# Experts: Silu on ScalarE, clip and sum on GpSimd, features on partitions in the down projection, token weights spread through DRAM

## The chip, the core and the metric

The kernel runs on one core of a Trainium2 chip. The metric is the device time of one execution in microseconds (us). TensorE is written PE below, VectorE DVE, ScalarE ACT, GpSimd POOL and SyncE SP.

## What is computed

The input x has 8 sequences of 512 tokens with 128 features. The reference, cut to what matters here:

```python
h = _layernorm(x) * (1 + ca) + sa
x = x + ga * attn(h)             # gates by softmax, then a scan over the 512 time steps
h = _layernorm(x) * (1 + cb) + sb
# ffn(h): 8 experts, 4 of them chosen per token
logits = x @ router_weight.T + router_bias
topk_w = softmax(top_k(logits, 4))
combine = zeros((N, E)).at[arange(N)[:, None], topk_idx].set(topk_w)
gate_up = einsum('nd,ejd->nej', x, gate_up_proj) + gate_up_proj_bias
gate, up = split(gate_up, 2, axis=-1)
gate = minimum(gate, 7.0)
up = clip(up, -7.0, 7.0)
act = (up + 1.0) * gate * sigmoid(1.702 * gate)
out = einsum('nei,edi->ned', act, down_proj) + down_proj_bias
y = einsum('ned,ne->nd', out, combine)
x = x + gb * y
```

Every expert is computed for every token; the weights of the experts that a token did not choose are 0. An expert has 256 hidden features. All data are float32.

## The kernel before

**Tiles.** A tile is 16 time steps of all 8 sequences, 128 tokens. There are 32 tiles. Four tiles make a superchunk (512 tokens, `NW`), and there are 8 superchunks.

**The stages.** `ln1(s)` normalises a superchunk. `gates(c)` makes the softmax gates of a tile: five matmuls (L220), for each a maximum and a subtraction on DVE (L224, L226) and an Exp on ACT (L229); then a sum, a reciprocal and a product over 2176 elements on DVE (L234, L235, L238). Eight DMAs from SP's queue (L243, 136 KB each) carry the gates to a layout with one row per head and sequence. `scan(c)` runs the 16 steps of a tile on DVE, one product (L256) and one sum (L259) per step, each waiting for the one before. `attn_out(c)` carries the states back with eight small DMAs (L269) and multiplies by W_out. `attn_post(s)` adds the residual, normalises, and makes the router: logits (L300), ranks, and the token weights `comb` (L338), tokens on partitions. It then transposes `comb` on PE (L345), copies it to `cT` (L347), and starts `y` with the weighted output biases (L350, L355).

**The experts.** `experts(s, es)` works through pairs of expert e and half ic of its 256 features, 16 to a superchunk. `front` issues two matmuls of 128x512 (gate L365, up L367), copies both from PSUM with their biases on ACT (L371, L373), and takes the Sigmoid of the gate copy (L375). `back` clips up on DVE (L382), multiplies by the limited gate (L383) and by the limited Sigmoid (L384); the result is `act`. `down` multiplies by the down projection with `act` as the stationary operand, so that tokens lie on the partitions of the output: 4 blocks of tokens times 2 halves, 8 matmuls of 128 columns (L391), each of which the profile shows as two instructions. Its PSUM tile `pd` has a single buffer (`ps_dn`, bufs=1). `combine` adds the output to `y` with the token weight as a per-partition scalar, four instructions on DVE (L399):

```python
nc.vector.scalar_tensor_tensor(
    y[:, k, :], pd[:, k, :], comb[:, k, e : e + 1], y[:, k, :], ALU.mult, ALU.add
)
```

`finish` multiplies `y` by the modulation row (L427), adds `x1` (L428), and stores (L431). The final `y` is tokens by features.

**What sets the order.** The functions are generators. Beside the scan of tile c the main loop advances `attn_out(c - 1)`, `ln1`, `gates(c + 2)` and a quarter of the experts of the superchunk before. From this text a scheduler makes a fixed order for each engine when the kernel is built, with an estimate of each instruction's length; it also places the waits, and each engine then works through its own list strictly in order. In the built order the experts of a superchunk do not lie evenly beside the scan: they stand together in a burst after `comb`, with a few scan steps between them, and the gates and most scan steps follow. A DMA is issued from the list of the engine that its line names, and a wait before it holds up that list. The DMAs of SP and ACT share eight completion semaphores in turn, so that a DMA also waits for the one that used its semaphore last.

Of the kernel before, what the change touches and what calls it, by code (L numbers as in the profile page):

```python
# [9 lines left out]
F32 = mybir.dt.float32  # L10
AF = mybir.ActivationFunctionType
ALU = mybir.AluOpType
AX = mybir.AxisListType

P = 128
EPS = 1e-5
ALPHA = 1.702
LIMIT = 7.0
TOP_K = 4
SIG_MAX = 1.0 / (1.0 + math.exp(-ALPHA * LIMIT))  # L20

# [7 lines left out]
def adaln_block_kernel(  # L29
    ctx: ExitStack,  # L30
    tc: tile.TileContext,
    x: bass.AP,        # [B, T, D]
    norm_w: bass.AP,   # [D, 1]
    wa_t: bass.AP,     # [D, H*M*(M+1)]
    wv_t: bass.AP,     # [D, D]
    wo_t: bass.AP,     # [D, D]
    rw_t: bass.AP,     # [D, E]
    r_bias: bass.AP,   # [1, E]
    gu_t: bass.AP,     # [D, E*2I]
    gu_bias: bass.AP,  # [128, E*4]  # L40
    dn_t: bass.AP,     # [E, I, D]
    dn_bias: bass.AP,  # [E, D]
    c_in: bass.AP,     # [B, D]
    w_mod: bass.AP,    # [D, 6*D]
    out: bass.AP,      # [B, T, D]
):
# [24 lines left out]
    ps_gu = ctx.enter_context(tc.tile_pool(name="ps_gu", bufs=3, space=PS))  # L71
    ps_dn = ctx.enter_context(tc.tile_pool(name="ps_dn", bufs=1, space=PS))
    ps_misc = ctx.enter_context(tc.tile_pool(name="ps_misc", bufs=2, space=PS))

    def misc_psum(name):
        return ps_misc.tile([P, 512], F32, tag="misc", name=name)

# [1 line left out]
    c_sb = const.tile([B, D], F32, name="c_sb")  # L79
# [31 lines left out]

# [1 line left out]
    ident = const.tile([P, P], F32, name="ident")  # L113
# [11 lines left out]
    )  # L125
    # up's bias with the 1 of (up + 1)
    ub1_sb = const.tile([P, E, IC], F32, name="ub1_sb")
    nc.vector.tensor_scalar(ub1_sb, gub_sb[:, :, IC:], 1.0, None, ALU.add)

# [1 line left out]
    sig_c = const.tile([B, D], F32, name="sig_c")  # L131
# [8 lines left out]
    for half in range(2):  # L140
# [5 lines left out]
            start=True, stop=True,  # L146
# [11 lines left out]
    def mod_row(i):  # L158
        return mod[:, i, :].unsqueeze(1).to_broadcast([P, KT, D])

# [1 line left out]
    def layernorm(dst, src, scale_i, shift_i, tag):  # L162
# [23 lines left out]
    f_tiles = {}      # superchunk -> what the experts need  # L186

# [96 lines left out]
    def attn_post(s):  # L284
        r = r_tiles.pop(s)
        x1 = sc_p.tile([P, KT, D], F32, tag="x1", name=f"x1_{s}")
        nc.vector.tensor_tensor(r, r, mod_row(2), ALU.mult)
        nc.vector.tensor_tensor(x1, r, x_sb[:, s * KT : (s + 1) * KT, :], ALU.add)
        h2 = sc_p.tile([P, KT, D], F32, tag="h2", name=f"h2_{s}")
        yield from layernorm(h2, x1, 4, 3, "b")  # L290
# [5 lines left out]
        yield  # L296
        # router: top 4 of 8, softmax over the chosen
        pr = misc_psum(f"pr{s}")
# [42 lines left out]
        yield  # L341
        # the experts' output biases, weighted
        pc = misc_psum(f"pc{s}")
# [3 lines left out]
        nc.scalar.copy(cT, pc[:E, :])  # L347
        pb = misc_psum(f"pb{s}")
        for k in range(KT):
            nc.tensor.matmul(  # L350
                pb[:, k * D : (k + 1) * D], cT[:, k * P : (k + 1) * P], dnb_sb,
                start=True, stop=True,
            )
        y = sc_p.tile([P, KT, D], F32, tag="y", name=f"y{s}")
        nc.scalar.copy(y.rearrange("p k d -> p (k d)"), pb)  # L355
        f_tiles[s] = (x1, h2T, comb, y)
        yield

    def experts(s, es):
        x1, h2T, comb, y = f_tiles[s]  # L360
        acts = {}

        def front(e, ic):
            pgt = ps_gu.tile([P, NW], F32, tag="gu", name=f"pgt{s}_{e}_{ic}")
            nc.tensor.matmul(pgt, gu_sb[:, e, ic * P : (ic + 1) * P], h2T, start=True, stop=True)  # L365
            pup = ps_gu.tile([P, NW], F32, tag="gu", name=f"pup{s}_{e}_{ic}")
            nc.tensor.matmul(  # L367
                pup, gu_sb[:, e, I + ic * P : I + (ic + 1) * P], h2T, start=True, stop=True
            )
            gt = ffn_p.tile([P, NW], F32, tag="gate", name=f"gate{s}_{e}_{ic}")  # L370
            nc.scalar.activation(gt, pgt, AF.Identity, bias=gub_sb[:, e, ic : ic + 1])  # L371
            up = ffn_p.tile([P, NW], F32, tag="up", name=f"up{s}_{e}_{ic}")
            nc.scalar.activation(up, pup, AF.Identity, bias=ub1_sb[:, e, ic : ic + 1])  # L373
            sg = ffn_p.tile([P, NW], F32, tag="sg", name=f"sg{s}_{e}_{ic}")
            nc.scalar.activation(sg, gt, AF.Sigmoid, scale=ALPHA)  # L375
            return gt, up, sg

        def back(e, ic, gt, up, sg):
            if ic == 0:
                acts[e] = ffn_p.tile([P, IC, NW], F32, tag="act", name=f"act{s}_{e}", bufs=2)  # L380
            # clip(up, -7, 7) + 1, min(gate, 7), sigmoid(1.702 min(gate, 7))
            nc.vector.tensor_scalar(up, up, 1.0 - LIMIT, 1.0 + LIMIT, ALU.max, ALU.min)  # L382
            nc.vector.scalar_tensor_tensor(up, gt, LIMIT, up, ALU.min, ALU.mult)  # L383
            nc.vector.scalar_tensor_tensor(acts[e][:, ic, :], sg, SIG_MAX, up, ALU.min, ALU.mult)  # L384

        def down(e):
            act = acts.pop(e)
            pd = ps_dn.tile([P, KT, D], F32, tag="pd", name=f"pd{s}_{e}")
            for k in range(KT):
                for ic in range(IC):  # L390
                    nc.tensor.matmul(  # L391
                        pd[:, k, :], act[:, ic, k * P : (k + 1) * P], dn_sb[:, e * IC + ic, :],
                        start=(ic == 0), stop=(ic == IC - 1),
                    )
            return pd

        def combine(e, pd):
            for k in range(KT):
                nc.vector.scalar_tensor_tensor(  # L399
                    y[:, k, :], pd[:, k, :], comb[:, k, e : e + 1], y[:, k, :], ALU.mult, ALU.add  # L400
                )

        waiting, downs = None, None
        for e in es:
            for ic in range(IC):
                made = (e, ic, *front(e, ic))
                yield
                if downs is not None:
                    combine(*downs)
                    downs = None  # L410
                if waiting is not None:
                    back(*waiting)
                    if waiting[1] == IC - 1:
                        downs = (waiting[0], down(waiting[0]))
                waiting = made
                yield
        back(*waiting)
        if downs is not None:
            combine(*downs)
        downs = (waiting[0], down(waiting[0]))  # L420
        yield
        combine(*downs)
        yield

    def finish(s):
# [81 lines left out]
```

## Time and profile before

| | us |
|---|---|
| median of the runs before | 1391.12 (three runs, 1390.35 to 1391.66) |
| span of the profiled execution | 1390.6 |
| DVE busy | 1151.2 (83%) |
| PE busy | 675.7 (49%) |
| ACT busy | 462.8 (33%) |
| POOL busy | 1.1 |
| DMA of the gates, g<-ee, in the chain of work that ended last | 15% of the span |

The profiled execution is one run of its own; its span, from the first to the last instruction, is 0.5 us under the median of the timed runs. The page divides the span in 40 slices and gives the busy share of each engine in tenths, lists groups of equal instructions with their busy time, mean length and the idle time just before them, and follows the chain of work that ended last back from the end. PE's busy time is that of pipelined matmuls whose ends are modelled: two matmuls of 0.59 us each may start 0.43 us apart.

### The profile page before, as it was taken

The numbers are of one execution on the slowest core, as the hardware profiler recorded it, in microseconds if no ns is written. First come the engines' busy times: TensorE is split into PE (matmuls) and PEld (weight loads), VectorE is DVE, ScalarE is ACT, GpSimd is POOL, SyncE is SP. The second block draws the span as 40 slices with busy tenths as digits, with TensorE's granted clock in tenths as the row PEclk, the third lists the DMA queues.
The fourth block names the chain that finished last, engine by engine and source line by source line (L and its number), as shares of the span: only waits on it lengthen the run. The fifth ranks groups of instructions, "written<-read, shape, count | busy, mean of one in ns | idle before, by whom it ended". The sixth has DMA issues, their size and how long they took to land.

```text
span 1390.6 us, 9491 instructions
## 1 busy us (share of the span) xinstructions
PE 675.7 (49%) x2181; PEld 348.3 (25%) x2181; DVE 1151.2 (83%) x2533; ACT 462.8 (33%) x850; POOL 1.1 (0%) x10
## 2 busy tenths in 40 slices
PE   1415049531594237830496315942369414771077
PEld 0101015310262014510153102620135201440044
DVE  3889699996999799996989969897898978888366
ACT  2401037320382115610373203821146102541054
POOL 0000000000000000000000000000000000000000
PEclk9755568865697667965688656976569756795579
DMA  6251514024330325005140242303241041501200
GB/s 199 32 60 14 60 21 49 1 32 45 36 31 10 44 25 65 2 11 63 20 51 0 30 48 33 34 10 38 31 50 17 10 54 20 61 1 21 24 0 8
DMA packets 80248, 47.39 MB, mean 34 GB/s; under 512 B 38064, under 2 KB 79296, under 8 KB 79936
## 3 DMA queue, kind: packets, MB, share of 16 engines
q1 hardware_dynamic: 78640, 42.03, 25.8%
q10 hardware_dynamic: 1552, 4.75, 1.0%
q14 instruction: 38, 0.31, 0.1%
q8 instruction: 18, 0.29, 0.1%
HBM read 6.91 MB, written 2.10 MB: 6 GB/s over the span
## 4 chain that ended last, share of the span: by engine, by line
DVE 40%; PE 32%; DMA 21%; issue 2%; SPq 2%; ACT 2%; DVEq 0%; ACTq 0%
DMA g<-ee 15%; PE pgt L365 9%; PE pd L391 8%; DVE g L256 8%; PE pup L367 8%; DVE ys L259 7%; DVE mx L224 5%; DVE z L234 5%; DMA yt<-ys 4%; PE pg L220 4%; DVE ee L226 4%; DVE ee L238 3%; SPq L243 2%; DVE z L235 2%; DMA x_sb<-in_x_dram 1%
## 5 line engine op out<-in xcount | busy, mean ns | idle before, releaser
L256 DVE TENSOR_TENSOR g<-g,ys 64x256 f32<-64x256 f32 x511 | 211.2, 413 | 107.0 <-DMA g<-ee 60.1
L220 PE MATMUL pg<-wav,hnT 128*128 128x459 f32 (+2 forms) x320 | 221.6, 815 | 133.5 <-DVE ee L226 108.7
L259 DVE TENSOR_REDUCE ys<-g 64x16 f32<-64x272 f32 x512 | 217.1, 424 | 11.3
L273 PE MATMUL py<-ident,yt 128*128 128x128 f32 x32 | 13.7, 427 | 436.5 <-DMA yt<-ys 435.8
L275 ACT COPY ytT<-py 128x128 f32<-128x128 f32 x32 | 8.5, 266 | 513.1 <-PE py L273 513.1
L391 PE MATMUL pd<-dn_sb,act 128*128 128x128 f32 x1024 | 146.6, 291 | 29.8 <-DVE act L384 16.2
L391 PEld LDWEIGHTS pd<-dn_sb,act 128*128 128x128 f32 x1024 | 136.2, 201 | 91.3 <-DVE act L384 36.6
L229 ACT ACTIVATE ee<-ee 128x459 f32<-128x459 f32 (+2 forms) x160 | 89.1, 564 | 201.4 <-DVE ee L226 179.6
L365 PE MATMUL pgt<-h2T,gu_sb 128*128 128x512 f32 x256 | 145.9, 654 | 0.0
L367 PE MATMUL pup<-h2T,gu_sb 128*128 128x512 f32 x256 | 138.8, 625 | 0.0
L220 PEld LDWEIGHTS pg<-wav,hnT 128*128 128x128 f32 x320 | 68.9, 254 | 257.2 <-issue 163.1
L273 PEld LDWEIGHTS py<-ident,yt 128*128 128x128 f32 x32 | 6.2, 193 | 461.3 <-issue 302.2
L224 DVE TENSOR_REDUCE mx<-pg 128x27 f32<-128x459 f32 (+2 forms) x160 | 95.1, 594 | 13.5 <-PE pg L220 12.8
L373 ACT ACTIVATE up<-pup,ub_sb 128x512 f32<-128x512 f32 x128 | 86.8, 678 | 40.8 <-PE pup L367 40.8
L371 ACT ACTIVATE gate<-pgt,gub_sb 128x512 f32<-128x512 f32 x128 | 87.6, 684 | 24.7 <-PE pgt L365 24.2
L226 DVE TENSOR_TENSOR ee<-pg,mx 128x459 f32<-128x459 f32 (+2 forms) x160 | 95.2, 595 | 0.0
L384 DVE SCALAR_TENSOR_TENSOR act<-sg,up 128x512 f32<-128x512 f32 x128 | 88.1, 688 | 7.4 <-ACT sg L375 3.4
L383 DVE SCALAR_TENSOR_TENSOR up<-gate,up 128x512 f32<-128x512 f32 x128 | 88.0, 688 | 2.9
L399 DVE SCALAR_TENSOR_TENSOR y<-pd,comb,y 128x128 f32<-128x128 f32 x256 | 74.9, 342 | 14.2 <-PE pd L391 13.9
L375 ACT ACTIVATE sg<-gate 128x512 f32<-128x512 f32 x128 | 80.5, 629 | 2.5
L234 DVE TENSOR_REDUCE z<-ee 128x128 f32<-128x2176 f32 x32 | 76.8, 2400 | 0.5 <-ACT ee L229 0.5
L238 DVE TENSOR_TENSOR ee<-ee,z 128x2176 f32<-128x2176 f32 x32 | 76.9, 2404 | 0.0
(89 smaller groups left out, 599.1 us busy)
## 6 DMA issues: line engine op xcount, KB each, us to landing
g<-ee SPq DMA_DIRECT2D x256, 136.0 KB
yt<-ys SPq DMA_DIRECT2D x256, 8.0 KB
x_sb<-in_x_dram SPq DMA_DIRECT2D x32, 64.0 KB
gu_sb<-in_gu_t_dram ACTq DMA_DIRECT2D x1, 2048.0 KB
out_dram<-y SPq DMA_DIRECT2D x32, 64.0 KB
wav<-in_wa_t_dram ACTq DMA_DIRECT2D x1, 1088.0 KB
wmod_sb<-in_w_mod_dram ACTq DMA_DIRECT2D x1, 384.0 KB
wo_sb<-in_wo_t_dram SPq DMA_DIRECT2D x1, 64.0 KB
```

The source lines that it names most:

```text
L220: nc.tensor.matmul(pg[:, :w], hnT, wav[:, g0 * J : g0 * J + w], start=True, stop=True)
L224: nc.vector.tensor_reduce(mx[:, g0 : g0 + n], pg3, AX.X, ALU.max)
L226: nc.vector.tensor_tensor(e3, pg3, mx[:, g0 : g0 + n].unsqueeze(2).to_broadcast([P, n, J]), ALU.subtract)
L229: nc.scalar.activation(e3, e3, AF.Exp)
L234: nc.vector.tensor_reduce(z, ee, AX.X, ALU.add)
L238: nc.vector.tensor_tensor(ee, ee, z.unsqueeze(2).to_broadcast([P, NG, J]), ALU.mult)
L256: nc.vector.tensor_tensor(a, a, prev.unsqueeze(1).to_broadcast([H * B, M, M]), ALU.mult)
L259: nc.vector.tensor_reduce(ys[:, t, :], g[:, t, :, :], AX.X, ALU.add)
L365: nc.tensor.matmul(pgt, gu_sb[:, e, ic * P : (ic + 1) * P], h2T, start=True, stop=True)
L367: nc.tensor.matmul(pup, gu_sb[:, e, I + ic * P : I + (ic + 1) * P], h2T, start=True, stop=True)
L384: nc.vector.scalar_tensor_tensor(acts[e][:, ic, :], sg, SIG_MAX, up, ALU.min, ALU.mult)
L391: nc.tensor.matmul(pd[:, k, :], act[:, ic, k * P : (k + 1) * P], dn_sb[:, e * IC + ic, :], start=(ic == 0), stop=(ic == IC - 1),)
```

## The change

Seven things change together. (1) ACT takes the Silu of 1.702 times the gate straight from PSUM, with a bias scaled by 1.702 when the kernel starts; the copy of the gate and the Sigmoid go. The limit on the gate becomes a limit on the Silu, and the factor 1.702 that is then too much is divided out of the token weights. (2) The clip of up moves to POOL. (3) On DVE one product per half is left. (4) The down projection has its weights as the stationary operand, so features lie on the partitions of the output and all 512 tokens in its columns: 2 matmuls of 512 columns per expert. (5) The token weights now differ along the columns and are equal in all partitions. They are transposed as before, divided by 1.702 (`cA`), written to DRAM (`cD`, 16 KB) and read back into all 128 partitions (`wB`, 2 MB), both from ACT's queue. (6) Each expert's output is multiplied by its row of `wB` on DVE; POOL adds the products up in `yT`. (7) `finish` turns `yT` back by matmuls with the identity and adds the output biases in the same PSUM tile. Besides, `x1` takes the place of `r`, and some tiles have other numbers of buffers. Comments and blank lines also changed; the diff without them:

```diff
-SIG_MAX = 1.0 / (1.0 + math.exp(-ALPHA * LIMIT))
+SILU_MAX = ALPHA * LIMIT / (1.0 + math.exp(-ALPHA * LIMIT))
...
+    dram = ctx.enter_context(tc.tile_pool(name="dram", bufs=2, space=bass.MemoryType.DRAM))
...
+    gb_sb = const.tile([P, E, IC], F32, name="gb_sb")
+    nc.vector.tensor_scalar(gb_sb, gub_sb[:, :, :IC], ALPHA, None, ALU.mult)
...
-        x1 = sc_p.tile([P, KT, D], F32, tag="x1", name=f"x1_{s}")
-        nc.vector.tensor_tensor(x1, r, x_sb[:, s * KT : (s + 1) * KT, :], ALU.add)
-        h2 = sc_p.tile([P, KT, D], F32, tag="h2", name=f"h2_{s}")
+        nc.vector.tensor_tensor(r, r, x_sb[:, s * KT : (s + 1) * KT, :], ALU.add)
+        x1 = r
+        h2 = sc_p.tile([P, KT, D], F32, tag="h2", name=f"h2_{s}", bufs=1)
...
         cT = small.tile([E, NW], F32, tag="cT", name=f"cT{s}")
         nc.scalar.copy(cT, pc[:E, :])
-        pb = misc_psum(f"pb{s}")
-        for k in range(KT):
-            nc.tensor.matmul(
-                pb[:, k * D : (k + 1) * D], cT[:, k * P : (k + 1) * P], dnb_sb,
-                start=True, stop=True,
-            )
-        y = sc_p.tile([P, KT, D], F32, tag="y", name=f"y{s}")
-        nc.scalar.copy(y.rearrange("p k d -> p (k d)"), pb)
-        f_tiles[s] = (x1, h2T, comb, y)
+        cA = ffn_p.tile([P, NW], F32, tag="w", name=f"cA{s}", bufs=2)
+        nc.scalar.mul(cA[:E, :], pc[:E, :], 1.0 / ALPHA)
+        cD = dram.tile([E, NW], F32, tag="cD", name=f"cD{s}")
+        nc.scalar.dma_start(cD, cA[:E, :])
+        wB = sc_p.tile([P, E, NW], F32, tag="wB", name=f"wB{s}", bufs=1)
+        nc.scalar.dma_start(wB, cD.rearrange("e n -> (e n)").unsqueeze(0).to_broadcast([P, E * NW]))
+        f_tiles[s] = (x1, h2T, cT, wB)
...
-            gt = ffn_p.tile([P, NW], F32, tag="gate", name=f"gate{s}_{e}_{ic}")
-            nc.scalar.activation(gt, pgt, AF.Identity, bias=gub_sb[:, e, ic : ic + 1])
-            up = ffn_p.tile([P, NW], F32, tag="up", name=f"up{s}_{e}_{ic}")
+            sg = ffn_p.tile([P, NW], F32, tag="sg", name=f"sg{s}_{e}_{ic}")
+            nc.scalar.activation(sg, pgt, AF.Silu, bias=gb_sb[:, e, ic : ic + 1], scale=ALPHA)
+            up = ffn_p.tile([P, NW], F32, tag="up", name=f"up{s}_{e}_{ic}", bufs=5)
             nc.scalar.activation(up, pup, AF.Identity, bias=ub1_sb[:, e, ic : ic + 1])
-            sg = ffn_p.tile([P, NW], F32, tag="sg", name=f"sg{s}_{e}_{ic}")
-            nc.scalar.activation(sg, gt, AF.Sigmoid, scale=ALPHA)
-            return gt, up, sg
+            nc.gpsimd.tensor_scalar(up, up, 1.0 + LIMIT, 1.0 - LIMIT, ALU.min, ALU.max)
+            return sg, up
...
-            nc.vector.tensor_scalar(up, up, 1.0 - LIMIT, 1.0 + LIMIT, ALU.max, ALU.min)
-            nc.vector.scalar_tensor_tensor(up, gt, LIMIT, up, ALU.min, ALU.mult)
-            nc.vector.scalar_tensor_tensor(acts[e][:, ic, :], sg, SIG_MAX, up, ALU.min, ALU.mult)
+            nc.vector.scalar_tensor_tensor(up, sg, SILU_MAX, up, ALU.min, ALU.mult)
+            acts.setdefault(e, []).append(up)
...
-            pd = ps_dn.tile([P, KT, D], F32, tag="pd", name=f"pd{s}_{e}")
-            for k in range(KT):
-                for ic in range(IC):
-                    nc.tensor.matmul(
-                        pd[:, k, :], act[:, ic, k * P : (k + 1) * P], dn_sb[:, e * IC + ic, :],
-                        start=(ic == 0), stop=(ic == IC - 1),
-                    )
+            pd = ps_dn.tile([P, NW], F32, tag="pd", name=f"pd{s}_{e}")
+            for ic in range(IC):
+                nc.tensor.matmul(
+                    pd, dn_sb[:, e * IC + ic, :], act[ic],
+                    start=(ic == 0), stop=(ic == IC - 1),
+                )
...
-            for k in range(KT):
-                nc.vector.scalar_tensor_tensor(
-                    y[:, k, :], pd[:, k, :], comb[:, k, e : e + 1], y[:, k, :], ALU.mult, ALU.add
-                )
+            if e == 0:
+                yT_tiles[s] = sc_p.tile([P, NW], F32, tag="yT", name=f"yT{s}", bufs=1)
+                nc.vector.tensor_tensor(yT_tiles[s], pd, wB[:, e, :], ALU.mult)
+                return
+            w = ffn_p.tile([P, NW], F32, tag="w", name=f"w{s}_{e}", bufs=2)
+            nc.vector.tensor_tensor(w, pd, wB[:, e, :], ALU.mult)
+            nc.gpsimd.tensor_tensor(yT_tiles[s], yT_tiles[s], w, ALU.add)
...
-        x1, _, _, y = f_tiles.pop(s)
-        nc.vector.tensor_tensor(y, y, mod_row(5), ALU.mult)
+        x1, _, cT, _ = f_tiles.pop(s)
+        yT = yT_tiles.pop(s)
+        pb = misc_psum(f"pb{s}")
+        for k in range(KT):
+            blk = slice(k * P, (k + 1) * P)
+            nc.tensor.matmul(pb[:, blk], yT[:, blk], ident, start=True, stop=False)
+            nc.tensor.matmul(pb[:, blk], cT[:, blk], dnb_sb, start=False, stop=True)
+        y = sc_p.tile([P, KT, D], F32, tag="y", name=f"y{s}", bufs=1)
+        nc.vector.tensor_tensor(
+            y, pb.rearrange("p (k d) -> p k d", d=D), mod_row(5), ALU.mult
+        )
         nc.vector.tensor_tensor(y, y, x1, ALU.add)
```

More of the change, by code (lines that the diff above doesn't have):

```diff
@@ L186, in adaln_block_kernel @@
     f_tiles = {}
+    yT_tiles = {}
     def ln1(s):
@@ L347, in attn_post @@
         nc.scalar.copy(cT, pc[:E, :])
-        pb = misc_psum(f"pb{s}")
-        for k in range(KT):
-            nc.tensor.matmul(
-                pb[:, k * D : (k + 1) * D], cT[:, k * P : (k + 1) * P], dnb_sb,
-                start=True, stop=True,
-            )
-        y = sc_p.tile([P, KT, D], F32, tag="y", name=f"y{s}")
-        nc.scalar.copy(y.rearrange("p k d -> p (k d)"), pb)
-        f_tiles[s] = (x1, h2T, comb, y)
+        cA = ffn_p.tile([P, NW], F32, tag="w", name=f"cA{s}", bufs=2)
[5 more added lines that the diff above has]
+        f_tiles[s] = (x1, h2T, cT, wB)
         yield
     def experts(s, es):
-        x1, h2T, comb, y = f_tiles[s]
+        x1, h2T, cT, wB = f_tiles[s]
         acts = {}
@@ L373, in front @@
             nc.scalar.activation(up, pup, AF.Identity, bias=ub1_sb[:, e, ic : ic + 1])
-            sg = ffn_p.tile([P, NW], F32, tag="sg", name=f"sg{s}_{e}_{ic}")
-            nc.scalar.activation(sg, gt, AF.Sigmoid, scale=ALPHA)
-            return gt, up, sg
[L378 to L384, printed above, removed]
+            nc.gpsimd.tensor_scalar(up, up, 1.0 + LIMIT, 1.0 - LIMIT, ALU.min, ALU.max)
@@ L386, in down, with back @@
+            return sg, up
+        def back(e, ic, sg, up):
+            nc.vector.scalar_tensor_tensor(up, sg, SILU_MAX, up, ALU.min, ALU.mult)
+            acts.setdefault(e, []).append(up)
         def down(e):
             act = acts.pop(e)
-            pd = ps_dn.tile([P, KT, D], F32, tag="pd", name=f"pd{s}_{e}")
-            for k in range(KT):
-                for ic in range(IC):
-                    nc.tensor.matmul(
-                        pd[:, k, :], act[:, ic, k * P : (k + 1) * P], dn_sb[:, e * IC + ic, :],
-                        start=(ic == 0), stop=(ic == IC - 1),
-                    )
+            pd = ps_dn.tile([P, NW], F32, tag="pd", name=f"pd{s}_{e}")
[4 more added lines that the diff above has]
+                )
```

## The prediction

> **What bounds the kernel now.** I began with the busy line and the 40 slices of the profile page.
>
> ```profile
> PE 675.7 (49%) x2181; PEld 348.3 (25%) x2181; DVE 1151.2 (83%) x2533; ACT 462.8 (33%) x850; POOL 1.1 (0%) x10
> ...
> PE   1415049531594237830496315942369414771077
> ...
> DVE  3889699996999799996989969897898978888366
> ```
>
> VectorE (DVE) is busy 83% of the span and GpSimd (POOL) not at all, so moving work from the first to the second looks like a gain. But TensorE (PE) rises to 9 or 10 tenths once per superchunk: the experts run as a burst. I therefore read the timeline of superchunk 2 (counted from 0) and cut it at three marks: the end of `comb` (L338) at 541.90 us, the first combine (L399) at 549.46, the end of the last at 591.08. The next `comb` ends at 705.96. Busy time in these three stretches (columns: stretch, length, PE, PEld, DVE, ACT, POOL, PE clock, DMA share, GB/s):
>
> ```profile
> 541.90:549.50 7.60, 7.60 (x38) 4.80 (x37) 6.34 (x15) 6.12 (x11) 0.00 (x0) 0.97 0.58 74
> 549.50:591.00 41.50, 36.67 (x167) 23.35 (x166) 37.99 (x98) 29.92 (x54) 0.00 (x0) 0.96 0.11 14
> 591.00:705.90 114.90, 39.87 (x70) 15.64 (x71) 97.30 (x204) 22.35 (x44) 0.00 (x0) 0.62 0.29 34
> ```
>
> A period is 7.6 + 41.5 + 114.9 = 164.0 us. In the last 114.9 us the experts have nothing to do but the final two additions. Only the first 49.1 us are open to this change, and there PE is as full as DVE: 44.3 us of 49.1. The last superchunk, after the scan, shows the burst alone. Its end, in the chain of work that ended last (start, length, what):
>
> ```profile
> 1375.99 1.23 PE pd L391 x11
> 1377.22 0.88 PE pup L367 x2
> 1378.09 0.02 issue
> 1378.12 0.70 ACT up L373
> 1378.81 0.02 issue
> 1378.84 0.44 DVE up L382
> 1379.28 0.02 issue
> 1379.30 0.70 DVE up L383
> 1380.00 0.02 issue
> 1380.03 0.70 DVE act L384
> 1380.73 0.04 issue
> 1380.77 1.84 PE pd L391 x14
> ```
>
> Up to the last expert the chain there is PE matmul on PE matmul. ACT and DVE appear only at the very end.
>
> [...] yt (8 KB) stands in the chain with 1.9 us. [...] with PE nearly idle from 581.6 to 586.1, the clock reads 0.50 from 587 to 590.
>
> **The change part by part.** Groups used (busy us, mean ns):
>
> ```profile
> L384 DVE SCALAR_TENSOR_TENSOR act<-sg,up 128x512 f32<-128x512 f32 x128 | 88.1, 688 | 7.4 <-ACT sg L375 3.4
> L383 DVE SCALAR_TENSOR_TENSOR up<-gate,up 128x512 f32<-128x512 f32 x128 | 88.0, 688 | 2.9
> L399 DVE SCALAR_TENSOR_TENSOR y<-pd,comb,y 128x128 f32<-128x128 f32 x256 | 74.9, 342 | 14.2 <-PE pd L391 13.9
> ```
>
> DVE. Clip (L382, 128 x 423 ns = 54.2 us), first product (L383, 88.0) and combine (L399, 74.9) go: 217 us. Sixty-four products of 128x512 with one PSUM operand come; the nearest rows are 620 ns for 459 elements from PSUM and 688 from SBUF, so 0.68 x 64 = 43.5. Net -174 us of DVE, 21.7 per superchunk. All of it lies in the burst (and the wait for PE is there too), not in the 114.9 us.
>
> ACT. Gate copy (87.6) and Sigmoid (80.5) become one Silu from PSUM, 128 x 684 ns = 87.6: -80 us. The copy of y (0.56) is replaced by cA (0.57). The built order has 58 table loads for 54, +4 x 1.28 us. ACT has 36 us of work in 49: no gain on the path.
>
> PE. An expert's down projection takes 16 short instructions at 0.11 us (14 in 1.56 us) and will take 4 long ones at 0.43 (a pair of pgt lasts 0.86): 1.78 to 1.72 us. No gain worth counting. In `finish` come 8 matmuls per superchunk for 4 removed; they stand among the gates, where PE is busy 39.9 of 114.9 us, and cost nothing except in the last superchunk.
>
> POOL. [...] The clip stands in the place of L382 and L383 (1.1 us), so the chain from ACT to the down projection keeps its length. [...]
>
> The broadcast. This is the new wait. `comb` is transposed, copied twice on ACT, written to DRAM (16 KB), read back into 128 partitions (2 MB); the first combine waits for it, and it stands only some 13 to 18 DVE instructions after `comb`. From the end of `comb`:
> - transposes end at +2.6 (before: 544.56); they keep their place behind a gate matmul.
> - cT and cA, 0.57 each, then up(1,0) 0.68, which stands before the DMA on ACT: +4.6. Issue 0.5 (rows of 0.3 to 0.9 at the start), landing 1.9: +7.0.
> - The read stands on ACT behind Silu(1,1), whose matmul stands behind the first down projection: that begins at +4.5, takes 1.7, the matmul 0.86, Silu 0.69: +7.8. Issue 0.4: +8.2.
> - 2 MB: gu_sb has this size, shape and queue. In its load, 12 to 18 us, 342 GB/s moved on average: 6.1 us, and 1.9 fixed: 8.0. Best, at the 483 GB/s of its fastest microsecond, 6.2; worst 11.6, the time until the next DMA of that queue went out. The gate transfer of the same moment (SP's queue, share 0.58) shares engines, but the built order reuses completion semaphores so that its third and fourth eighths wait for the write and the read; its tile is scanned only after the burst.
> - Landing: +16.2, with bounds +13.5 and +21 (ACT or POOL later).
>
> Before, the first combine was at +7.6. What waits behind it: everything on DVE, in order; and the second down projection, since `pd` has one buffer. PE gets to it at about +10.5 (five matmuls after the first), stops for 6 us, and falls to half clock.
>
> After the landing: product 0.68; on PE 14 down and 21 gate/up matmuls x 0.857 = 30.0; half clock for some 5 us, +2.5; last expert's ACT, POOL, DVE chain 2.3; last product 0.68; handovers 0.3. Sum 36.5. So the last combine ends at 16.2 + 36.5 = +52.7 instead of +49.1: **+3.6 us per superchunk**, x 7 = 25.
>
> In the 114.9 us nothing changes: by the built order DVE has 90.8 us there for 91.0. Last superchunk: `comb` at 1336.52, combines from 1345.90 to 1383.78 (+9.4 to +47.3). Landing about +15, then 36 matmuls 30.9 + 6.5 = 37.4: +52.4, 5 us later. Then one addition on POOL 1.3 and 8 matmuls 1.8 ahead of the last two DVE steps: 3. Total 25 + 5 + 3 = **+33 to +34 us**. Against the profiled execution (span 1390.6; its time is within 0.5 us of the median 1391.12) that is 1425.
>
> **The rivals.**
> 1. *The broadcast is hidden* (the other side, faster). If the data land by the time PE gets to the second down projection (+10.5), PE keeps its clock and no longer waits for DVE: 10.5 + 0.7 + 30.0 + 2.3 + 1.0 = +44.5, -4.6 x 7 = -32 us, and the end about even: 1359. The point of decision is a landing at about +11.5. For it: DVE stood in PE's way for some 7 us of this burst. Against: two DMAs in series and ACT's queue leave little below +13.5.
> 2. *GpSimd becomes the bound*. Clips of 2 us and additions of 2.3 [...] make 40 us for the 12 clips and 7 additions after the landing, against 35: +5 x 8 more, about 1470. [...]
> 3. *DVE alone is the bound*: its 174 us come off, about 1220. Against: the chain in the last burst, and 41.5 us in which PE was busy 36.7.
>
> **How the numbers follow.** The wait decides: 0.62, 1425, own range 1402 (landing at +13.5) to 1463 (at +21). GpSimd as bound: 0.14, up to 1500. Hidden: 0.17, 1355 to 1388. DVE alone: 0.03. Wait and relief cancel: 0.04. A measurement tells about 0.2% (2.8 us) from no change. Slower 0.62 + 0.14 - 0.01 = 0.75; same 0.04; faster 0.21. The range from 1370 to 1485 leaves out DVE alone, the lower part of hidden and the upper of GpSimd, about 0.15.
>
> **What would show it.** Right: DVE's first combine waits for a DMA of wB for 5 us or more in each superchunk; it starts 14 to 18 us after `comb`; PE has a gap of about 6 us there and clock 0.5 after it; 115 us from last combine to next `comb`; DVE busy about 980 us. Wrong: no such wait; or clips over 1.5 us with DVE products waiting for POOL; or the 115 us changed, by scan steps that POOL holds up.

## The result, and the profile after

The changed kernel takes 1437.22 us (median of four runs, 1431.53 to 1446.18); beside it the kernel before took 1391.39 (1390.35 to 1393.91). The ratio is 1.0332, with a 95% interval from 1.0289 to 1.0375: slower, by 46 us where 34 were forecast. The profiled execution is the longest of the four, 9 us above the median; its span is 1444.5 us, 53.9 above that of the profile before.

The busy line and two rows of the 40 slices, as shown of before:

```profile
PE 728.7 (50%) x1477; PEld 308.4 (21%) x1477; DVE 1018.0 (70%) x2086; ACT 403.3 (28%) x726; POOL 162.7 (11%) x194
...
PE   1414058634585145940677325851568406681277
...
DVE  3799694877939786696857979397774968567442
```

DVE lost 133 us of work and the kernel became slower. The three stretches of superchunk 2, now from comb at 560.84, the first product with `wB` at 574.30, the end of the last at 612.70 to the next comb at 734.11 (columns as in the prediction: stretch, length, PE, PEld, DVE, ACT, POOL, PE clock, DMA share, GB/s):

```profile
560.84:574.30 13.46, 8.38 (x23) 3.50 (x21) 5.45 (x15) 12.12 (x24) 2.56 (x4) 0.97 0.52 169
574.30:612.70 38.40, 34.46 (x72) 14.19 (x72) 22.53 (x42) 15.88 (x24) 15.92 (x17) 0.90 0.19 20
612.70:734.11 121.41, 51.89 (x90) 22.33 (x91) 98.60 (x203) 22.99 (x45) 2.49 (x2) 0.54 0.29 34
```

Before, they were 7.6, 41.5 and 114.9. The first is longer by 5.9 and the second shorter by 3.1: that is the wait and its relief. But the third, in which "nothing changes", is longer by 6.5, with 12 us more of PE at a clock of 0.54.

The wait itself, on DVE and then on PE (start, length, what; in brackets the idle time of the engine before it and what ended it):

```profile
574.31 0.69 DVE L402 TENSOR_TENSOR yT<-pd,wB 128x512 f32<-128x512 f32 x1 [5.51 <-DMA wB<-cD]
...
575.06 3.78 PE L393 MATMUL pd<-up,dn_sb 128*128 128x512 f32 x4 [5.83 <-DVE yT L402]
```

The groups that took the place of L384, L383 and L399, with the GpSimd groups:

```profile
L381 POOL TENSOR_SCALAR up<-up 128x512 f32<-128x512 f32 x128 | 86.4, 675 | 1114.5 <-ACT up L379 1111.1
...
L386 DVE SCALAR_TENSOR_TENSOR up<-sg,up 128x512 f32<-128x512 f32 x128 | 94.4, 738 | 119.7 <-POOL up L381 119.4
...
L406 POOL TENSOR_TENSOR yT<-yT,w 128x512 f32<-128x512 f32 x56 | 75.1, 1342 | 154.7 <-DVE w L405 121.6
```

L386 seems to wait 119 us for GpSimd. A clip takes 0.68 us, though, and GpSimd itself waits 1111 us for ACT: it is only the last link of the chain from PE. In the last burst, once the weights have landed, PE runs without a gap up to the last expert, 5.15 us per expert (12 matmuls of 0.43), while "<-POOL" stands before nearly every L386.

The end, in the chain of work that ended last:

```profile
1429.21 1.14 PE pd L393 x2
1430.36 0.02 issue
1430.38 0.70 DVE w L405
...
1431.19 1.30 POOLq L518
1432.49 0.04 issue
1432.53 0.49 PE pb L437 x2
1433.02 0.41 PE pb L438 x2
1433.43 0.52 PE pb L437 x2
1433.95 0.72 PE pb L438 x2
1434.67 0.72 PE pb L437 x2
```

After the last product come the addition on GpSimd (1.30, which this view puts under L518) and eight matmuls of two instructions each. PE had stood idle for 2 us, and from the fourth matmul on a pair costs 0.72 instead of 0.4.

Where the 53.9 us lie, from the marks of all superchunks: first comb +1.0; seven bursts (comb to last combine) 366.8 for 346.1, **+20.7**; seven stretches from there to the next comb 799.5 for 772.8, **+26.7**; last burst -1.1; from its end to the end +6.6. These are the parts of the profiled execution; between the medians lie 46 us.

### The profile page after: what moved, and what is told of

The parts are those of the page before. It is cut to its first block, busy times and chain, and to the rows that moved or that the text cites. A ratio compares the mean times of both kernels' runs of the same rounds, so it can differ in the third digit from the quotient of the medians.

```text
span 1444.5 us, 7622 instructions
## 1 busy us (share of the span) xinstructions
PE 728.7 (50%) x1477; PEld 308.4 (21%) x1477; DVE 1018.0 (70%) x2086; ACT 403.3 (28%) x726; POOL 162.7 (11%) x194
## 4 chain that ended last, share of the span: by engine, by line
DVE 39%; PE 30%; DMA 24%; issue 3%; ACT 2%; SPq 1%; POOL 1%; POOLq 0%; ACTq 0%; DVEq 0%
DMA g<-ee 14%; DVE g L263 8%; DVE ys L266 8%; PE pg L227 7%; PE pd L393 6%; PE pgt L371 6%; PE pup L373 5%; DMA wB<-cD 5%; DVE z L241 4%; DVE mx L231 4%; DMA yt<-ys 4%; DVE ee L233 3%; DVE ee L245 3%; DVE up L386 2%; DVE z L242 1%
## 5 line engine op out<-in xcount | busy, mean ns | idle before, releaser
L227 PE MATMUL pg<-wav,hnT 128*128 128x459 f32 (+2 forms) x320 | 242.2, 879 | 126.0 <-DVE ee L233 100.8
L263 DVE TENSOR_TENSOR g<-g,ys 64x256 f32<-64x256 f32 x511 | 224.5, 439 | 107.0 <-DMA g<-ee 56.6
L266 DVE TENSOR_REDUCE ys<-g 64x16 f32<-64x272 f32 x512 | 217.3, 425 | 12.3
L280 PE MATMUL py<-ident,yt 128*128 128x128 f32 x32 | 13.2, 412 | 399.0 <-DMA yt<-ys 398.1
L381 POOL TENSOR_SCALAR up<-up 128x512 f32<-128x512 f32 x128 | 86.4, 675 | 1114.5 <-ACT up L379 1111.1
L393 PE MATMUL pd<-up,dn_sb 128*128 128x512 f32 x256 | 144.3, 669 | 68.5 <-DVE yT L402 45.0
L386 DVE SCALAR_TENSOR_TENSOR up<-sg,up 128x512 f32<-128x512 f32 x128 | 94.4, 738 | 119.7 <-POOL up L381 119.4
L227 PEld LDWEIGHTS pg<-wav,hnT 128*128 128x128 f32 x320 | 75.9, 279 | 247.3 <-issue 152.7
L377 ACT ACTIVATE sg<-pgt,gb_sb 128x512 f32<-128x512 f32 x128 | 87.9, 687 | 105.7 <-PE pgt L371 105.3
L231 DVE TENSOR_REDUCE mx<-pg 128x27 f32<-128x459 f32 (+2 forms) x160 | 95.3, 595 | 29.4 <-PE pg L227 29.1
L379 ACT ACTIVATE up<-pup,ub_sb 128x512 f32<-128x512 f32 x128 | 87.6, 685 | 81.4 <-PE pup L373 81.3
L280 PEld LDWEIGHTS py<-ident,yt 128*128 128x128 f32 x32 | 6.0, 186 | 426.7 <-issue 298.9
L406 POOL TENSOR_TENSOR yT<-yT,w 128x512 f32<-128x512 f32 x56 | 75.1, 1342 | 154.7 <-DVE w L405 121.6
L393 PEld LDWEIGHTS pd<-up,dn_sb 128*128 128x128 f32 x256 | 49.6, 205 | 145.9 <-DVE up L386 56.5
L373 PEld LDWEIGHTS pup<-h2T,gu_sb 128*128 128x128 f32 x256 | 53.5, 212 | 68.5 <-issue 66.6
```

What stands on the lines that cost most here:

```text
L227: nc.tensor.matmul(pg[:, :w], hnT, wav[:, g0 * J : g0 * J + w], start=True, stop=True)
L231: nc.vector.tensor_reduce(mx[:, g0 : g0 + n], pg3, AX.X, ALU.max)
L263: nc.vector.tensor_tensor(a, a, prev.unsqueeze(1).to_broadcast([H * B, M, M]), ALU.mult)
L266: nc.vector.tensor_reduce(ys[:, t, :], g[:, t, :, :], AX.X, ALU.add)
L373: nc.tensor.matmul(pup, gu_sb[:, e, I + ic * P : I + (ic + 1) * P], h2T, start=True, stop=True)
L386: nc.vector.scalar_tensor_tensor(up, sg, SILU_MAX, up, ALU.min, ALU.mult)
```

## The experiments

Bursts and stretches are the sums over the first seven superchunks in the profiled execution. A profiled execution lies up to 13 us from its kernel's median: the changed kernel's 9 above, e2's 13 above, n1's 11 below. The ratio is to the kernel before on the same chip.

| kernel | median us | ratio, 95% interval | bursts | stretches |
|---|---|---|---|---|
| before | 1391.4 | | 346.1 | 772.8 |
| changed | 1437.2 | 1.0332 [1.0289, 1.0375] | 366.8 | 799.5 |
| e1 no finish matmuls | 1421.5 | 1.0220 [1.0201, 1.0239] | 371.0 | 774.5 |
| e2 no broadcast | 1403.2 | 1.0108 [1.0064, 1.0152] | 300.7 | 832.4 |
| e3 before + 8 matmuls | 1422.6 | 1.0238 [1.0218, 1.0257] | 347.3 | 795.2 |
| w1 transfer, no wait | 1400.2 | 1.0056 [1.0042, 1.0071] | 308.7 | 802.6 |
| e12 neither | 1393.7 | 1.0017 [1.0008, 1.0027] | 303.8 | 815.0 |
| f1 finish at the burst's end | 1452.2 | 1.0450 [1.0431, 1.0468] | 368.9 | 803.4 |
| f2 f1 + read in two | 1433.4 | 1.0299 [1.0249, 1.0348] | 340.8 | 819.4 |
| n1 no GpSimd | 1426.4 | 1.0255 [1.0237, 1.0273] | 357.4 | 782.1 |
| n2 sum on VectorE | 1427.4 | 1.0275 [1.0221, 1.0329] | 353.9 | 794.9 |
| e5 Silu alone | 1399.9 | 1.0055 [1.0036, 1.0075] | 335.2 | 786.2 |
| e4 Silu, clip on GpSimd | 1385.8 | 0.9961 [0.9946, 0.9976] | 325.0 | 785.1 |
| g1 e4, factor in comb | 1381.7 | 0.9925 [0.9910, 0.9940] | 325.0 | 786.2 |

### The matmuls of finish: e1 and e3

```diff
-            nc.tensor.matmul(pb[:, blk], yT[:, blk], ident, start=True, stop=False)
-            nc.tensor.matmul(pb[:, blk], cT[:, blk], dnb_sb, start=False, stop=True)
...
-            y, pb.rearrange("p (k d) -> p k d", d=D), mod_row(5), ALU.mult
+            y, yT.rearrange("p (k d) -> p k d", d=D), mod_row(5), ALU.mult
```

> The changed kernel without the eight matmuls of finish: yT goes to the modulation as it lies, so the last turn of the layout and the output biases are left out. Theory A (the stretch from the last combine to the next comb grew from 111-115 us to 113-121 because these eight matmuls, 0.44 us an instruction at half clock, stand among the gates of a tile, and the gates wait for PE there): that stretch goes back to 113 to 115 us in every superchunk and the tail loses some 5 us: about 1437 - 27 - 5 = 1405 us. Rival B (the stretch grew because GpSimd's additions hold up scan steps, L263 439 ns instead of 413): only the tail's 5 us go, 1432. Rival C (the clock lost in the broadcast wait carries on into that stretch): also about 1432.

Measured: 1421.5, 16 us less than the changed kernel in the medians and 27 in the profiled executions. The stretches are 113.3 to 115.3 us (89.7 for the last of the seven), their sum is 774.5, within 2 us of before, and the part after the last burst is 5.2 us shorter. The stretch of superchunk 2 (it was 114.9 before, 121.4 in the changed kernel):

```profile
606.33:721.18 114.85, 42.98 (x76) 17.34 (x77) 97.34 (x201) 23.25 (x46) 1.87 (x2) 0.58 0.29 35
```

So the eight matmuls are what lengthened the stretch; the total is not as low as 1405, since the bursts grew by 4 us and the changed kernel's median lies below its profile.

e3 adds the same eight matmuls to the kernel before:

```diff
-        nc.vector.tensor_tensor(y, y, mod_row(5), ALU.mult)
+        pb = misc_psum(f"pf{s}")
+        for k in range(KT):
+            blk = slice(k * P, (k + 1) * P)
+            nc.tensor.matmul(pb[:, blk], y[:, k, :], ident, start=True, stop=False)
+            nc.tensor.matmul(pb[:, blk], ident[:E, :], dnb_sb, start=False, stop=True)
+        nc.vector.tensor_tensor(
+            y, pb.rearrange("p (k d) -> p k d", d=D), mod_row(5), ALU.mult
+        )
```

> The kernel before with eight matmuls added in finish, as the changed kernel has them there (four by the identity, four of 8 rows), so that the output is turned and biases are added twice. Theory A: about 4 us in the stretch after the burst of seven superchunks and 4 at the end: 1391 + 32 = 1423 us. Rivals B and C: no GpSimd and no broadcast are in this kernel, so only the tail's 4 us: 1395.

Measured: 1422.6; the stretches grew by 22.4, the bursts by 1.2. Thirty-one microseconds for eight short matmuls per superchunk, with no GpSimd and no broadcast in the kernel: rivals B and C are not needed for it. The stretches of superchunks 1 and 2:

```profile
428.12:541.13 113.01, 43.14 (x87) 18.33 (x88) 97.52 (x203) 22.61 (x44) 0.00 (x0) 0.62 0.29 36
591.61:712.50 120.89, 47.68 (x88) 20.95 (x89) 97.55 (x203) 22.74 (x45) 0.00 (x0) 0.60 0.29 33
```

Why so much, and why in the second and not in the first? In the changed kernel's own trace superchunks 2 and 3 likewise do the same work at different clocks. The 20 us around their `pb` matmuls:

```profile
684.40:704.40 20.00, 18.04 (x37) 9.28 (x38) 14.04 (x31) 4.60 (x12) 0.00 (x0) 0.53 0.08 16
852.20:872.20 20.00, 13.24 (x38) 6.50 (x38) 18.44 (x37) 4.60 (x12) 0.00 (x0) 0.80 0.09 18
```

At a clock of 0.53 PE is busy 18.0 of 20 us, and DVE gets 14.0 us of work done; at 0.80 it is 13.2 and 18.4. The stretch around the first was 121.4 us, around the second 112.8. PE has been idle before it (36.9 us ahead of L280 at 684.40), then meets gates, `pb` and gates in one row, and DVE's L231 and L440 wait for it. Before the second place PE had been idle nearly as long, 34.6 us; there the clock was back at 1.00 after 5.4 us, in the first place after 18.8. What decides this, no run here shows.

The same split goes through every kernel measured whose order has DVE's usual work in the stretch and these matmuls among the gates. Its six full stretches, in us, by the clock granted during the eight matmuls:

| kernel | clock 0.50 | clock 0.85 to 1.00 |
|---|---|---|
| changed | 121.2, 121.4, 121.0, 119.5 | 115.3, 112.8 |
| e3 | 120.9, 117.8, 120.9, 121.3 | 111.6, 113.0 |
| w1 | 120.9, 121.7, 123.1 | 115.0, 113.5, 116.2 |
| n1 | 119.6 | 115.9, 115.4, 112.4, 115.2, 114.9 |
| n2 | 120.9, 121.0 | 116.8, 116.8, 113.5, 116.4 |

Without the matmuls these stretches are 111.2 to 115.0 (before) and 113.3 to 115.3 (e1). At full clock the eight matmuls thus cost little, at half clock some 6 us. How many of the six stretches meet the half clock is not the same in every kernel's profile, so sums of stretches from single executions are to be compared with this in mind.

The forecast's own profile showed the place; these are windows of the kernel before:

```profile
663.10:669.10 6.00, 3.67 (x7) 1.97 (x8) 5.59 (x15) 0.92 (x3) 0.00 (x0) 0.50 0.10 12
669.10:675.10 6.00, 5.59 (x10) 1.92 (x8) 5.22 (x12) 1.99 (x5) 0.00 (x0) 0.50 0.01 1
```

In the second of them PE is 93% busy at half clock: no room for six more microseconds.

### Another place for them: f1

In the text `finish` follows the experts directly. Its PSUM tile comes from a pool that `py`, `ph` and `po` of later tiles use in turn, and in the built order `pb` stands behind them. f1 takes it from the pool of `pd`:

```diff
-        pb = misc_psum(f"pb{s}")
+        pb = ps_dn.tile([P, NW], F32, tag="pd", name=f"pb{s}")
```

> The changed kernel with one edit: the PSUM tile of finish comes from the pool of the down projection instead of the one that the gates' and router's small tiles use in turn. In the built order the eight matmuls then stand at the end of the burst and no longer among the gates of a later tile. Theory A (their place among the gates, at half clock, is what lengthens the stretch): the stretch from the last combine to the next comb goes from 113 to 121 us back to 113 to 116, and the time to 1418 to 1428 us, near the 1421 of the kernel without these matmuls. Rival E (the eight matmuls cost the same wherever they stand): 1437.

Measured: 1452.2, a miss of theory A as written and worse than rival E's 1437. The matmuls stand right behind the burst, but they have to wait for GpSimd's last addition, and DVE's list has L440 there (who waits for what: us in total, times, longest):

```profile
DVE y L440 <- PE pb L438: 35.2, 8, 7.4
...
PE pb L437 <- POOL yT L406: 17.9, 8, 2.5
```

PE idles 2.2 us for the sum, then does the eight matmuls at half clock (0.50 us an instruction); DVE, with scan steps behind L440, idles 3.8 us for them. The six full stretches are 117.8 to 119.6. So what costs is not the place among the gates as such: in both places DVE's list waits for matmuls at half clock, and behind the burst they cost 4 us per superchunk (stretches 803.4 against e1's 774.5). In f1 they run at 0.50 in all eight superchunks; a stretch of 112.8 like superchunk 3's above does not occur. That fits a median 15 us above the changed kernel's, though the profiled spans differ by only 4.3: the changed kernel's profile is its longest run. The mean clock of f1's four runs was 0.691 to 0.695, that of the changed kernel's profiled run 0.691 and of its other three 0.698 to 0.701; how it lay in their stretches is not shown.

### The broadcast: e2, w1, e12, f2

e2 drops the transfer and the wait:

```diff
-        cA = ffn_p.tile([P, NW], F32, tag="w", name=f"cA{s}", bufs=2)
...
-        nc.scalar.dma_start(wB, cD.rearrange("e n -> (e n)").unsqueeze(0).to_broadcast([P, E * NW]))
+    wB = const.tile([P, E, NW], F32, name="wB")
+    nc.scalar.dma_start(wB, gu_t.rearrange("p (e j) -> p e j", e=E))
```

> The changed kernel with wB loaded once at the start, from other data of the same size, and cA, cD and the read of 2 MB left out, so the products use wrong token weights. Theory A (the wait for the broadcast, 5.5 us of DVE and some 6 of PE per superchunk, is what lengthens the burst): the first product starts about 8.5 us after comb, the last combine ends 45 to 47 us after comb instead of 52, the stretch after it stays at 113 to 121 us: about 1437 - 8 x 6 = 1389 us. Rival C (the clock lost in the wait carries on): the later stretch shrinks too, to 115: about 1365. Rival D (GpSimd's clip sets the pace of the burst): last combine still at 50 or more, about 1425.

Measured: 1403.2, 34 us less than the changed kernel. The bursts fall from 52 to 42-44, but the stretches grow by 33 in sum (in an execution 13 us above the median). The built order shows the main reason: it had put 21 to 24 scan instructions into the burst, and with no wait there it puts 10 to 14, so that DVE has 102 to 104 us of work in each full stretch instead of 98 to 99. Neither a plain A nor C. So I kept the transfer and took the wait alone, by letting the products read one constant row:

```diff
-            nc.vector.tensor_tensor(w, pd, wB[:, e, :], ALU.mult)
+            nc.vector.tensor_tensor(w, pd, wC, ALU.mult)
```

> The changed kernel with cA, cD and the read of 2 MB as they are, but the products read one row of other data loaded at the start, so nothing waits for the read and the token weights are wrong. If the wait is all of the broadcast's price: as the kernel without any broadcast, 1403 us, within 6. If the transfer itself costs (the gates' DMAs share its engines and its completion semaphores): between 1410 and 1437, with longer waits for the gates (g) in the stretch after the burst.

Measured: 1400.2. Superchunk 2 in the same three stretches:

```profile
552.35:556.98 4.63, 4.63 (x15) 2.10 (x14) 4.07 (x12) 4.17 (x13) 1.33 (x2) 1.00 0.09 13
556.98:597.81 40.83, 36.62 (x81) 14.33 (x79) 22.54 (x46) 23.53 (x33) 17.27 (x19) 0.97 0.33 74
597.81:719.53 121.72, 48.75 (x92) 21.49 (x93) 99.31 (x204) 23.34 (x45) 2.49 (x2) 0.60 0.29 34
```

Five of the seven superchunks keep 21 or 22 scan instructions in the burst (the changed kernel 22 to 24), and the bursts last 41.4 to 46.9; the stretch is as long as with the wait, 121.7. So **the wait is worth 37 us in the medians, the transfer nothing that shows**, and the clock lost in the wait does not carry over (rival C falls again). The 37 are rather too few: the row that w1 loads at the start is issued from ACT's list at 29.96 us, ACT's first activation (the Sigmoid of the condition) follows at 31.63 instead of 25.66, and the first comb ends at 224.0 instead of 218.7. e2 and e12, with such a load too, have their first comb at 223.7.

> The changed kernel without the broadcast (other data in its place, loaded at the start) and without the eight matmuls of finish: both edits tried before, together. If their prices add (34 us for the one, 16 in the medians and 27 in the profiled executions for the other): 1376 to 1387 us, with the stretch after the burst below 118 us. If they overlap (each only removes a wait that the other then takes over): 1398 or more.

Measured: 1393.7, between the two expectations. With neither, each burst holds 8 to 10 scan instructions and DVE has 102 to 103 us in each full stretch. The two prices don't add, since what leaves the burst comes back on DVE behind it. Even then the kernel is not faster than before; without the 5 us of the added load I estimate 1389, about as fast.

f2 reads the weights of experts 0 and 1 first, on top of f1's edit:

```diff
-        wB = sc_p.tile([P, E, NW], F32, tag="wB", name=f"wB{s}", bufs=1)
+        for n, (e0, e1) in enumerate(((0, 2), (2, E))):
+            wB.append(sc_p.tile([P, e1 - e0, NW], F32, tag=f"wB{n}", name=f"wB{n}_{s}", bufs=1))
```

> The edit of the run before, and the weights read back in two DMAs, experts 0 and 1 first (512 KB), then the other six. Theory A (it is the length of the 2 MB read, 8 us from issue to the first product, on which DVE and PE stand): the first product starts about 9.5 us after comb instead of 13.5, PE keeps its clock, the last combine ends at 47 to 48 instead of 52; some scan steps lose their place in the wait, which gives about 2 us per superchunk back: 1395 to 1408 us. Rival F (the fixed time of the two DMAs in series is what counts, or both reads share the engines and land together): first product at 12 or later, 1418 to 1428.

Measured: 1433.4, 19 less than f1. The first product starts 10.2 to 11.1 us after comb instead of 14.3 to 15.1: in superchunk 2 the 512 KB land 3.8 us after the end of their issue, where 2 MB took 8.1. The mechanism is theory A's, in part: the bursts lose 28 us, but only four of the seven end 46 to 48 us after comb, where PE's clock is 0.97 to 1.00; the others take 50 to 51, at 0.90 to 0.93. And 16 of the 28 come back in the stretches, and the start was f1's 1452, so 1395 to 1408 is missed.

### GpSimd: n1 and n2

```diff
-            nc.gpsimd.tensor_scalar(up, up, 1.0 + LIMIT, 1.0 - LIMIT, ALU.min, ALU.max)
+            nc.vector.tensor_scalar(up, up, 1.0 + LIMIT, 1.0 - LIMIT, ALU.min, ALU.max)
...
-            nc.gpsimd.tensor_tensor(yT_tiles[s], yT_tiles[s], w, ALU.add)
+            nc.vector.tensor_tensor(yT_tiles[s], yT_tiles[s], w, ALU.add)
```

> The changed kernel with the clip and the sum on VectorE instead of GpSimd, nothing else. Rival B (GpSimd holds up VectorE's two-operand instructions): L263 falls from 439 to about 413 ns, and up to 13 us of VectorE's time come back. Theory A: the burst is bound by the wait and PE, so VectorE's 11 us more of work per superchunk (16 x 0.42 + 7 x 0.68) fit into the 25 us that it idles there: 1430 to 1440 us, the tail about 1 us shorter. If GpSimd had relieved a bound, this would cost some 8 x 5: above 1465.

Measured: 1426.4: with *more* work on DVE the kernel is 11 us faster, and the intervals of the two ratios don't meet. The profiled executions differ by 31, but 17 of these lie in the stretches, where n1's matmuls of `finish` met the half clock in one full stretch and the changed kernel's in four (table above). The rest, 13, is where GpSimd had its work or at the start: the bursts are 9.4 shorter, the last burst and the end 2.0, the time to the first comb 1.9. The scan's product before, in the changed kernel, and in n1:

```profile
L256 DVE TENSOR_TENSOR g<-g,ys 64x256 f32<-64x256 f32 x511 | 211.2, 413 | 107.0 <-DMA g<-ee 60.1
```

```profile
L263 DVE TENSOR_TENSOR g<-g,ys 64x256 f32<-64x256 f32 x511 | 224.5, 439 | 107.0 <-DMA g<-ee 56.6 <-DMA yt<-ys 37.8
```

```profile
L263 DVE TENSOR_TENSOR g<-g,ys 64x256 f32<-64x256 f32 x511 | 211.2, 413 | 106.7 <-DMA g<-ee 56.7 <-DMA yt<-ys 38.2
```

In the changed kernel 21 of the scan's products last longer beside GpSimd's work than their usual 0.41 us: 0.9 to 1.5 beside an addition, 0.8 beside a clip alone. L386, which like them has two inputs in SBUF, took 1.75 us instead of 0.69 in six places where an addition had begun just before it; in ten where L386 began first it kept its 0.68, and the addition took 1.57 instead of 1.26. L405, with one input in PSUM, stays at 0.67 to 0.69 us in the 15 cases in which GpSimd works beside it (clips, all of them), and the scan's sum, with one input, at 0.40 to 0.43 in 43 cases. n2 moves only the sum:

> The changed kernel with the sum on VectorE and the clip left on GpSimd. On the kernel before, the clip is worth more on GpSimd (1386) than on VectorE (1400); in the changed kernel taking both off GpSimd gains 11 us. If the sum of 1.27 us, which stands before clips in GpSimd's order and holds up VectorE, is what costs: 1415 to 1428 us, L263 back to 413-420 ns. If the clip is: 1433 or more.

Measured: 1427.4 (1423.2 to 1441.7); L263 420, L386 687 instead of 738. The sum is most of it by these lengths, but the interval of the ratio still touches the changed kernel's, so the split between sum and clip is not sharp.

### Parts alone: e4, e5, g1

On the kernel before, with `down` and `combine` left as they were:

```diff
-            gt = ffn_p.tile([P, NW], F32, tag="gate", name=f"gate{s}_{e}_{ic}")
-            nc.scalar.activation(gt, pgt, AF.Identity, bias=gub_sb[:, e, ic : ic + 1])
+            nc.scalar.activation(sg, pgt, AF.Silu, bias=gb_sb[:, e, ic : ic + 1], scale=ALPHA)
...
+            nc.gpsimd.tensor_scalar(up, up, 1.0 + LIMIT, 1.0 - LIMIT, ALU.min, ALU.max)
...
+            nc.vector.scalar_tensor_tensor(acts[e][:, ic, :], sg, SILU_MAX, up, ALU.min, ALU.mult)
```

> The kernel before with two parts of the change alone: Silu on ACT, and the clip on GpSimd with one product per half on DVE; tokens stay on the partitions in the down projection and comb stays a per-partition scalar (1/1.702 goes into the down weights at the start). Theory A: with neither broadcast nor finish matmuls the burst is bound by PE, 5.2 to 5.3 us per expert after a first combine at 7.5: last combine at 44.5 to 46 instead of 49.2, the rest as before: 1391 - 8 x 4 = 1360 us, 1355 to 1372. Rival D (GpSimd's clip sets the pace): 49 or more, 1391 or slower. Rival B (GpSimd holds up the scan steps): no gain in the burst beyond 1 us, 1385.

Measured: 1385.8. The bursts did fall, to 44.3 to 47.3, 21.1 in sum; the stretches grew by 12.3 and the first comb came 3.7 later, which left 5 of the 31 us expected. DVE has about 1 us more of work in each full stretch than before; why the stretch grows by nearly 2, I did not settle. e5 has the clip on DVE:

> The kernel before with the Silu alone: one product per half, the clip stays on VectorE. Theory A: the burst of the version with the clip on GpSimd is bound by PE (5.2 us per expert) with VectorE idle for 19 us of it, so the clip's 6.8 us per superchunk fit there, and no scan step is held up: 1380 to 1388 us, the same as with the clip on GpSimd or a little better. Rival: the clip on VectorE lengthens the chain from ACT to the down projection or VectorE's queue: 1390.

Measured: 1399.9, a miss: bursts of 47.4 to 48.6, and slower than before. The first comb comes 5.0 us later than before, and the stretches grow by 13.4 where the bursts lose 10.9. That the clip is worth 14 us on GpSimd here is measured; that it is so because the clip leaves the chain between ACT and the down projection is only argued. g1 drops the scaling of the down weights at the start:

```diff
-    nc.gpsimd.tensor_scalar(dn_sb, dn_sb, 1.0 / ALPHA, None, ALU.mult)
...
+        nc.scalar.mul(cw, comb, 1.0 / ALPHA)
```

> The kernel before with Silu on ACT and the clip on GpSimd, as in the run that gave 1386, but 1/1.702 goes into a copy of comb on ACT (128x32 per superchunk) instead of the down weights at the start, since the first comb came 3.7 us later there. If the scaling at the start did that: 1380 to 1384 us. If the later first comb is the order's: 1385 to 1388.

Measured: **1381.7, faster than both kernels**, than the kernel before by 0.75% (ratio 0.9925, from 0.9910 to 0.9940); the first comb is at 216.0 instead of 221.3. Its superchunk 2:

```profile
542.79:549.68 6.89, 6.89 (x37) 4.46 (x36) 4.98 (x13) 3.90 (x7) 1.52 (x2) 0.98 0.58 67
549.68:590.03 40.35, 37.15 (x169) 22.83 (x168) 23.82 (x68) 25.14 (x43) 7.99 (x13) 1.00 0.15 16
590.03:705.78 115.75, 39.71 (x72) 15.90 (x71) 98.17 (x205) 22.68 (x43) 0.61 (x1) 0.60 0.29 34
```

PE is nearly full in the burst and DVE idle for 18 us of it. More scan steps there may be the next gain; no run tried it.

## Why the prediction was right, and where it was wrong

- **Sign and mechanism: right.** L402 waits for the DMA of wB in every superchunk, 43.9 us in all, 5.2 to 7.0 in the first seven and 2.8 in the last. In superchunk 2 PE stands 5.83 us (forecast 6) and then needs 3.78 us for four matmul instructions that take 1.88 at full clock. w1 shows the wait to be the largest single cost, 37 us of the medians against e1's 16.
- **Landing: +13.5 for +16.2.** The read itself took 8.1 (forecast 8.0), but it began 2.7 us earlier, at +5.1. The transposes of `comb` ended at +1.5 (forecast +2.6), and both DMAs went out while the ACT instruction ahead of them was still running: L359 at 563.62 beside L379 from 563.50, L361 at 565.89 beside L377 from 565.83. The landing is at the forecast's lower bound.
- **After the landing: 38.4 for 36.5**, with PE at half clock for 5.2 us from its restart at 575.06 (forecast some 5); so the last combine ended at +51.9, forecast +52.7. Two errors cancel, which is luck. Sum over seven bursts: +20.7, forecast +25.
- **"In the 114.9 us nothing changes": wrong, the step that failed.** It cost 26.7 us in the profiled execution. The prediction put the eight matmuls of `finish` there at nothing, because PE is busy only 39.9 of 114.9 us. The share is that of the whole stretch; where they stand PE is full, and in four of six full stretches at half clock: these took 119.5 to 121.4 us, the other two 112.8 and 115.3. e1 takes 25 us back, e3 puts 22 into the kernel before. Counting DVE's work (90.8 against 91.0) could not show it: over the seven stretches DVE's work grew by 6.5 us, its idle time by 20. That the total, 46 for 34, is still near the forecast is in part luck: the bursts and the last superchunk cost less than forecast.
- **Last superchunk: -1.1 for +5.** Its landing came at +11.9, about rival 1's point of decision, and PE went on at full clock (0.99).
- **The tail: +6.6 for +3**: the matmuls took 5 us, not 1.8, most of them at half clock after the wait for GpSimd.
- **GpSimd.** A clip takes 0.68 us on average and a sum 1.34, 20.2 us per superchunk beside some 43 of PE. That GpSimd would not be the bound was only the author's estimate, since it did no such work before; rival 2's 2 and 2.3 us were suppositions. What VectorE would lose to it was taken as 0; n1, which gives the work back to DVE, gains 11 us in all, some 1.4 per superchunk.
- **DVE busy 1018, not 980.** Subtracting group by group gives 978. L263 and L386 grew by 13 and 6; the rest is the overlap of neighbouring records, which is counted once in the busy line and is lost with the neighbours.
- **Rival 1** (hidden, 1359) was mispriced by the same step: with the wait gone (w1) the bursts are as it said, 44.1 on average, but the total is 1400, of which the added load makes 5. **Rivals 2 and 3** fell: PE, not GpSimd or DVE, sets the pace of the burst, and DVE idles for 25 us of 52 on average.

## What to carry to other kernels

Price a moved instruction by the windows of its new place, some 5 us wide, at the clock that is there, and not by the busy share of the long stretch around it: eight short matmuls that "fit" cost the kernel before 31 us, the changed one 16. When work leaves a burst that another engine bounds, ask which work the order now puts elsewhere: in e2, e4, f2 and e12 half of what the bursts gained, or somewhat more, came back behind them, in w1, whose order kept its scan steps in most bursts, 3 of 58 us. An experiment that loads other data at the start pays for that load too, in w1 5 us before the first comb. Try the parts of a change alone: the first three of the seven made the kernel faster, and the rest ate it.

## What the runs showed of the hardware

- The same matmuls in the same place ran at a clock of 0.53 in one superchunk and 0.80 in the next (20 us windows), and 8.6 us of the stretch went with it. From 684.40 to 703.17 us the clock stayed at 0.50, with PE busy 17.5 of these 18.8 us. The changed kernel's four runs spread over 14.6 us, the kernel before's over 3.6; whether the clock makes this spread is not shown.
- A GpSimd addition of 128x512 (1.27 us) stretched a DVE product of 64x256 from 0.41 to 1.32 us (longest of all 1.48); a DVE product of 128x512 took up to 1.75 instead of 0.69. With one input in PSUM it stayed at 0.67 to 0.69 beside clips (0.61 and more); no addition ran beside such a product.
- DMAs in ACT's list were issued while the activation ahead of them still ran: L359 0.12 us and L361 0.06 us after the start of an activation of 0.66 to 0.69.
- A read of 16 KB in DRAM into 128 partitions (2 MB written) took 8.1 us, a quarter of it 3.8, both from the end of the issue to the landing.
